# Local q, k and v in products of 32 rows, and an opening in another order

## The chip, the cores and the metric

The kernel runs on one core of a Trainium2 chip. The metric is the device time of one execution in microseconds (us), lower is better. Before the change it is 1029.03 us, the median of three runs (1028.87 to 1030.4).

## The reference, cut to what matters

The input x is four images of 512 rows and 256 columns, all float32. Four steps follow, each on a layer-normed x and added to x:

```
x = x + window_attention(layernorm(x))
x = x + ffn(layernorm(x))
x = x + causal_attention(layernorm(x))
x = x + ffn(layernorm(x))

# window attention: tokens of 16 channels, on a grid of 128 x 64 an image
qkv = tok @ qkv_w                        # 16 -> 48
x1 = branch(first 8 channels of q, k, v, windows of 1 x 8 tokens)
x2 = branch(last 8 channels of q, k, v, windows of 8 x 1 tokens)
# a branch: softmax(q k^T / sqrt 8) v, plus a depthwise 3x3 convolution of v inside the window ("lepe")
att = concat(x1, x2) @ proj_w + proj_b
tok = tok + layernorm(att) * ln_w + ln_b

# ffn: 256 -> 2048 -> 256, 4-bit weights with scales
out = (gelu(x @ Wg.T) * (x @ Wu.T)) @ Wd.T
```

In a window of 1 x 8 only the middle row of a 3x3 filter meets other tokens, in one of 8 x 1 only the middle column: three taps each.

## The kernel before, in words

Five engines work side by side: PE (matrix products), DVE (vector), ACT (activations and copies), POOL, and SP, which only issues transfers. PE's result goes to PSUM, whose banks are handed out from three pools: `pair` gives two banks at once and has two such slots, used in turn; `one` gives a single bank; `fbank` gives the FFN three.

**Stages.** First comes the opening: constants, the window attention of image 0, and the first part of dequantising the FFN's weights. Then come three windows: in each, the first FFN of image b is woven with the window attention of image b + 1 (`beside_window`, L1276; woven by `weave`, L1110). Then the first FFN of image 3 and the second FFN of images 0 to 2 are woven with the causal attention of four images, and the second FFN of image 3 stands alone. The order of PE is written out by hand: `weave` takes a piece of the FFN for each 0.86 us that the other work asks for with its `yield`s, and a factor per window (L1284) stretches these. In the opening (L1196) PE, DVE and ACT all stand in the order of the calls. In the windows the order of DVE and ACT comes from a scheduler, apart from some dependences made by hand (`queue_behind`).

**Local attention of one image.** `window_load` (L223) brings 128 partitions of 8 tokens for each of 8 rows of tokens. `window_front` (L241) takes the statistics, normalises, transposes (`yTp`, L314), copies (`yT`, L321), and multiplies: for each of the 8 rows one product of all 128 rows of partitions (8 tokens of 16 channels) with a block-diagonal weight `bw` of 448 columns (q, k and v of both branches and the first branch's convolution), and one with `taps`, 64 columns for each of the two or three rows of tokens that the second branch's convolution reaches (L334, L336). Each pair of rows goes by one ACT copy into `T` (L344), the taps' bank by one more (L349). For image 0, `busy(12)` (L309) puts products of no use on PE ahead of the transposes. `window_parts` then has, for each branch and half: the products q k (`tq`, L400 and L408), their sum over channels by folds on DVE and by piles on PE (`sc`, L384), the maximum (`mx`), exponent, sums, shares, weighted values (`tv`, L475 and L483), their sum (`va` by PE, L496 by DVE) and `att`. `window_back` projects (`aTp`, L575 and L581; `pr`, `prw`, `ss`), takes the root by Newton steps, forms `z` (L599), which PE moves into the row layout (`zp`, L617), and `add` (L628) adds it to the rows `X`. `rows_shift` (L236) adds the bias ln_b to `X` beforehand, by four ACT operations an image.

**FFN.** `norm_rows` (L680) takes four row statistics (L686), their roots on POOL (`inv_root`, L92 and L93), normalises (`xn`, L700), transposes (`xTp`) and copies (`xT`). `ffn` (L733) has 16 blocks of a gate product (`pg`), an up product (`pu`), gelu on ACT (`gs`) and a product of both on DVE (`it`, L771), and after each eight blocks 32 down products (`po`), added to `X` (L792). All go through the three `fbank` banks, so a later `pg` or `pu` waits until `it` has read an earlier one. `behind_due` keeps the FFN's DVE work behind the image's `add`.

**Weights.** `dequant` (L635 to 668) is a stream of twelve blocks (g0, u0, g1, u1, d0 and so on) of six DVE operations, called words here; `some(words, n)` places n of them, and in window 1 `along` places four at each step of the attention. 24 words stand ahead of the first FFN's transposes.

## Time and profile before

| | us |
|---|---|
| median of three runs | 1029.03 |
| the profiled execution, its own time | 1029.56 |
| its span in the profile | 1027.8 |
| first FFN matmul | 78.33 |
| PE busy, 0 to 76 / 76 to 150 / 150 to the end | 67.97 / 67.24 / 870.83 |
| DVE busy, the same three | 65.52 / 73.90 / 529.86 |
| window 1: first and last piece of image 2's q, k, v | 161.09 to 169.50 |
| window 2: the same of image 3 | 262.9 to 271.85 |

A span is counted from the first to the last event that the profiler sees; the execution's own time has 1.8 us more around it. A row of "busy time by stage" gives a stretch's bounds and length, then for each engine the busy us with the number of instructions (PE, PE's weight loads, DVE, ACT, POOL), the granted clock, the transfer engines' share and GB/s. A group of instructions gives its line, engine, operation, names of output and inputs, shape and count, then busy us and the mean ns of one, then the idle time of that engine just before them and who ended it. [...] the busy times of its groups overlap, and starts tell more than durations. [...]

### The profile page before, as it was taken

Reading aid. Unit: us, or ns where it says so; the run is one execution under the profiler, and the core shown is the slowest. Engines: PE = TensorE matmul, PEld = TensorE weight load, DVE = VectorE, ACT = ScalarE, POOL = GpSimd, SP = SyncE. Lnnn points to the kernel's source line nnn. Section 1 sums busy time; section 2 is a strip of 40 time slices with the busy share of each in tenths; the row PEclk is TensorE's granted clock in tenths of the full one; section 3 lists DMA queues with packets and bytes.
Section 4 is the critical chain, followed back from the end, with each engine's and each line's share of the span. In section 5 each row is a group of like instructions: output and inputs, shape, how many; then the busy total and the mean of one; then the engine's idle time right before and its main releaser. Section 6 shows DMA issues by size and latency. Waiting matters only on the chain.

```text
span 1027.8 us, 13237 instructions
## 1 busy us (share of the span) xinstructions
PE 1006.0 (98%) x5054; PEld 587.9 (57%) x5054; DVE 669.3 (65%) x1570; ACT 350.2 (34%) x586; POOL 133.7 (13%) x261
## 2 busy tenths in 40 slices
PE   7999899999999999999999999999999999999998
PEld 6864656564756475464474554664644746446556
DVE  7989988847776777847477555776465575543111
ACT  2545222131212213435524445235254253461110
POOL 4100100000000012011330112311113201120000
PEclk9999999999999999999999999999999999999999
DMA  7310100000000020000000000000000000000000
GB/s 187 85 40 3 61 21 22 0 1 1 1 1 1 0 68 1 1 1 1 1 1 0 1 2 1 6 16 1 1 1 2 20 1 1 1 1 21 0 1 21
DMA packets 14399, 15.27 MB, mean 15 GB/s; under 512 B 2352, under 2 KB 10840, under 8 KB 14304
## 3 DMA queue, kind: packets, MB, share of 16 engines
q1 hardware_dynamic: 12416, 13.31, 4.4%
q10 hardware_dynamic: 1568, 1.06, 0.4%
q8 instruction: 40, 0.66, 0.3%
q14 instruction: 23, 0.19, 0.1%
q0 software_dynamic: 352, 0.06, 0.1%
HBM read 12.32 MB, written 2.10 MB: 14 GB/s over the span
## 4 chain that ended last, share of the span: by engine, by line
PE 87%; DVE 10%; DMA 1%; POOL 1%; issue 1%; SPq 0%; ACT 0%; ACTq 0%; POOLq 0%; DVEq 0%
PE pg_s L744 11%; PE pu_s L762 11%; PE po_s L779 11%; PE pu_f L762 9%; PE pg_f L744 9%; PE po_f L779 8%; PE s L936 5%; PE o L1021 4%; PE sT L985 4%; PE qkv_b L875 3%; PE qkv L334 2%; PE qkT L912 1%; PE qkv_b L879 1%; DVE tq L408 1%; PE zp L617 1%; DVE tq L389 1%
## 5 line engine op out<-in xcount | busy, mean ns | idle before, releaser
L951 DVE CUSTOM_DVE_ANT_0 junk<-s,mask 128x512 f32<-128x512 f32 (+3 forms) x256 | 110.1, 486 | 36.9 <-PE s L936 19.8
L762 PE MATMUL pu_f<-xT_f,u 128*128 128x512 f32 x256 | 122.9, 597 | 4.4 <-DVE it_f L771 4.1
L744 PE MATMUL pg_f<-xT_f,g 128*128 128x512 f32 x256 | 124.4, 599 | 2.9 <-ACT xT_f L723 1.4
L744 PE MATMUL pg_s<-xT_s,g 128*128 128x512 f32 x256 | 126.7, 603 | 0.0
L762 PE MATMUL pu_s<-xT_s,u 128*128 128x512 f32 x256 | 125.4, 601 | 0.0
L779 PE MATMUL po_f<-d,it_f 128*128 128x256 f32 x512 | 117.5, 381 | 0.6 <-DVE it_f L771 0.6
L779 PE MATMUL po_s<-d,it_s 128*128 128x256 f32 x512 | 118.0, 382 | 0.0
L779 PEld LDWEIGHTS po_s<-d,it_s 128*128 128x128 f32 x512 | 95.2, 190 | 20.8 <-issue 8.8
L779 PEld LDWEIGHTS po_f<-d,it_f 128*128 128x128 f32 x512 | 95.0, 190 | 18.4 <-issue 5.8
L1001 POOL TENSOR_SCALAR_AFFINE_SELECT e<-e 128x256 f32<-128x256 f32 x128 | 52.5, 422 | 344.9 <-ACT e L997 342.1
L997 ACT ACTIVATE e<-sT 128x1024 f32<-128x1024 f32 (+1 forms) x72 | 66.4, 968 | 72.0 <-PE sT L985 72.0
L762 PEld LDWEIGHTS pu_f<-xT_f,u 128*128 128x128 f32 x256 | 47.1, 190 | 61.0 <-issue 51.6
L744 PEld LDWEIGHTS pg_s<-xT_s,g 128*128 128x128 f32 x256 | 45.9, 190 | 56.8 <-issue 50.9
L762 PEld LDWEIGHTS pu_s<-xT_s,u 128*128 128x128 f32 x256 | 46.1, 190 | 54.4 <-issue 50.2
L744 PEld LDWEIGHTS pg_f<-xT_f,g 128*128 128x128 f32 x256 | 46.2, 190 | 53.6 <-issue 42.6
L753 DVE SCALAR_TENSOR_TENSOR g_s<-g_s,gs_s 128x512 f32<-128x512 f32 x48 | 33.1, 691 | 59.1 <-ACT g_s L752 58.5
L756 ACT ACTIVATE gs_f<-pg_f 128x512 f32<-128x512 f32 x48 | 28.5, 595 | 122.4 <-PE pg_f L744 109.7
L771 DVE TENSOR_TENSOR it_f<-pu_f,gs_f 128x512 f32<-128x512 f32 x48 | 32.6, 683 | 33.1 <-PE pu_f L762 33.1
L750 ACT COPY gs_s<-pg_s 128x512 f32<-128x512 f32 x48 | 28.1, 586 | 67.8 <-PE pg_s L744 67.6
L936 PE MATMUL s<-kT,qT 16*128 16x384 f32 (+3 forms) x512 | 50.0, 467 | 0.0
L792 DVE TENSOR_TENSOR X<-po_s,X 128x256 f32<-128x256 f32 (+1 forms) x33 | 13.5, 412 | 54.0 <-PE po_s L779 54.0
L1021 PE MATMUL o<-e,V 128*32 128x256 f32 (+3 forms) x512 | 44.4, 441 | 0.3 <-PE sT L985 0.3
(226 smaller groups left out, 1352.9 us busy)
## 6 DMA issues: line engine op xcount, KB each, us to landing
X<-in_x_dram SPq DMA_DIRECT2D x4, 512.0 KB
out_dram<-X SPq DMA_DIRECT2D x15, 128.0 KB
xa<-in_x_dram SPq DMA_DIRECT2D x28, 64.0 KB
pkg<-in_gate_p_dram SPq DMA_DIRECT2D x4, 256.0 KB
sbg<-in_gate_s_dram SPq DMA_DIRECT2D x4, 256.0 KB
pku<-in_up_p_dram SPq DMA_DIRECT2D x4, 256.0 KB
sbu<-in_up_s_dram SPq DMA_DIRECT2D x4, 256.0 KB
pkd<-in_down_p_dram SPq DMA_DIRECT2D x4, 256.0 KB
```

The source lines that it names most:

```text
L744: nc.tensor.matmul(pg, Wf["g"][par][q][:, o : o + P], xT[:, par, :], start=par == 0, stop=par == 1)
L753: nc.vector.scalar_tensor_tensor(g2, g2, 1.0, gs, ALU.add, ALU.mult)
L762: nc.tensor.matmul(pu, Wf["u"][par][q][:, o : o + P], xT[:, par, :], start=par == 0, stop=par == 1)
L771: behind_due(nc.vector.tensor_tensor(it, pu, gs, ALU.mult))
L779: nc.tensor.matmul(po[:, 0:W], inter[k][:, i * P : (i + 1) * P], Wf["d"][par][j // 2][:, (j % 2) * W : (j % 2 + 1) * W], start=k == 0, sto ...
L875: nc.tensor.matmul(ps[:, 0, :], xT[:, par, rows], c["wqk"][:, :, par], start=par == 0, stop=par == 1)
L936: nc.tensor.matmul(pss[hl // 2][:, hl % 2, at : at + n], qT[h0 : h0 + HD, g, i * P : (i + 1) * P], kT[h0 : h0 + HD, g, 0:n], start=True, s ...
L951: nc.vector.tensor_tensor_reduce(out=junk[:, 0:n], in0=pss[k][:, hl % 2, at : at + n], in1=c["mask"][:, 512 - n : 512], scale=1.0, scalar= ...
L985: nc.tensor.matmul(pss[hl // 2][:, hl % 2, at : at + n], kT[h0 : h0 + HD + 1, g, kt * P : (kt + 1) * P], qT[h0 : h0 + HD + 1, g, kt * P : ...
L997: nc.scalar.activation(e[:, :, 0 : 512 - at0], pss[k][:, :, at0:512], AF.Exp)
L1001: nc.gpsimd.affine_select(out=diag, in_=diag, pattern=[[0, 2], [1, P]], compare_op=ALU.is_ge, fill=0.0, base=0, channel_multiplier=-1,)
L1021: nc.tensor.matmul(outs[g][h0 : h0 + 32, kt * P : 512], v[:, kt, 4 * g + hl, :], e[:, hl % 2, at : at + n], start=kt == 0, stop=kt == 2,)
```

## The change

The weights of q, k and v now cover two tokens instead of eight: `bw` has 96 columns, the same in each group of 32 rows. For each half of an image (`hf`, four rows of tokens) 16 products of 32 rows, four beside each other in four groups of rows and four banks (both `pair` slots), give q, k and v; up to 20 more of 16 to 48 columns give the second branch's convolution in the same banks. After the first half, `across` gives the first branch's convolution by 8 products of all rows and 64 columns. An image has 80 products instead of 16, and `T` is laid out by halves and filled by eight copies and one, whose innermost runs have 2 or 16 elements. The operations of DVE that need both halves of the second branch (`tq` L408 and `tv` L483) become two each. `pw`, `lnw` and `z` use another order of channels.

In the opening, 8 words fewer stand ahead of the first FFN (6 instead of 15 at the first place, 1 more after the first product); `busy(12)` becomes `busy(8)`; image 1's transposes stand behind image 0's second projection instead of ahead of it; the 12 `rows_shift` operations of images 1 to 3 stand ahead of the root instead of after `zp`; image 1's second half stands behind `add`. The first `norm_rows` adds EPS on DVE instead of POOL.

In windows 1 and 2, the first half of the next image's q, k, v and `across` stand ahead of `zp`, the second half behind `add`, with other weights for the weaving. In the built program the causal part has the same order on each engine in both kernels. The second half's second pair of banks follows `zp` in the same slot.

```diff
-        bw = aw.tile([P, 7, 8, 8], F32, name="bw")
...
+        odd = aw.tile([P, 2], F32, name="odd")
+        nc.vector.tensor_reduce(odd, sh[:, 1, :].rearrange("p (r t) -> p t r", t=2), AX.X, ALU.add)
+        bw = aw.tile([P, 96], F32, name="bw")
+        nc.vector.tensor_tensor(
+            bw[:, 0:64].rearrange("p (e t) -> p e t", t=2), bcast(odd, 1, 32), bcast(wrep[:, 0:32], 2, 2), ALU.mult
+        )
...
+        taps = aw.tile([P, 3, 2, 8], F32, name="taps")
+        for t in range(3):
+            nc.vector.tensor_tensor(taps[:, t], bcast(odd, 2, 8), bcast(wc[:, 1, 2 - t, :], 1, 2), ALU.mult)
+        bl = aw.tile([P, 8, 8], F32, name="bl")
...
+        c.update(bw=bw, taps=taps.rearrange("p t j d -> p (t j d)"), bl=bl.rearrange("p j d -> p (j d)"))
...
-            busy(12)
+            busy(8)
...
-        T = a2.tile([P, 8, 8, 8, 8], F32, tag="T", name=f"T{b}")
-        lp = one(f"lepe{b}")
-        for u in range(4):
-            ps = pair(f"qkv{b}_{u}")
-            for a in range(2):
-                s = 2 * u + a
-                nc.tensor.matmul(ps[:, a, 0:448], yT[:, s, :], c["bw"], start=True, stop=True)
-                t0, t1 = (1 if s == 0 else 0), (2 if s == 7 else 3)
-                nc.tensor.matmul(
-                    lp[:, (s - 1 + t0) * 64 : (s - 1 + t1) * 64],
-                    yT[:, s, :],
-                    c["taps"][:, t0 * 64 : t1 * 64],
-                    start=s == 0,
-                    stop=s == 7,
-                    skip_group_check=True,
+
+        T = a2.tile([P, 2, 8, 4, 64], F32, tag="T", name=f"T{b}")
+        state[b] = (y, T)
+
+        def across():
+            lp = one(f"lepe{b}")
+            for s in range(8):
+                nc.tensor.matmul(lp[:, 64 * s : 64 * s + 64], yT[:, s, :], c["bl"], start=True, stop=True)
+            nc.scalar.copy(T[:, :, 7].rearrange("p h s e -> p h (s e)"), lp.rearrange("p (h e) -> p h e", h=2))
+
+        for hf in range(2):
+
+            pss = [pair(f"qkv{b}_{hf}_{k}") for k in range(2)]
+            lo, hi = 4 * hf, 4 * hf + 3
+            for s in range(lo, hi + 1):
+                for r in range(4):
+                    nc.tensor.matmul(
+                        pss[r // 2][:, r % 2, 0:384].rearrange("p (g s e) -> p g s e", g=6, s=4)[:, :, s - lo],
+                        yT[32 * r : 32 * r + 32, s, :],
+                        c["bw"][32 * r : 32 * r + 32, :],
+                        start=s == lo,
+                        stop=False,
+                        skip_group_check=True,
+                    )
+            for s in range(max(lo - 1, 0), min(hi + 1, 7) + 1):
+                t0, t1 = max(0, lo - s + 1), min(3, hi + 2 - s)
+                at = 384 + 16 * (s - 1 - lo)
+                for r in range(4):
+                    nc.tensor.matmul(
+                        pss[r // 2][:, r % 2, at + 16 * t0 : at + 16 * t1],
+                        yT[32 * r : 32 * r + 32, s, :],
+                        c["taps"][32 * r : 32 * r + 32, 16 * t0 : 16 * t1],
+                        start=False,
+                        stop=s == min(hi + 1, 7),
+                        skip_group_check=True,
+                    )
+            for k in range(2):
+                nc.scalar.copy(
+                    T[:, hf, 0:4].rearrange("p g s (d j) -> p (g s d) j", j=8)[:, :, 4 * k : 4 * k + 4].rearrange(
+                        "p n (r t) -> p n r t", t=2),
+                    pss[k][:, :, 0:256].rearrange("p r (n t) -> p n r t", t=2),
                 )
-            nc.scalar.copy(
-                T[:, 0:7, 2 * u : 2 * u + 2].rearrange("p g a j d -> p g a (j d)"),
-                ps[:, :, 0:448].rearrange("p a (g e) -> p g a e", g=7),
-            )
-            yield 0.5
-        nc.scalar.copy(T[:, 7].rearrange("p s j d -> p (s j d)"), lp)
-        state[b] = (y, T)
+            for k in range(2):
+                nc.scalar.copy(
+                    T[:, hf, 4:7].rearrange("p g s e -> p (g s) e")[:, :, 32 * k : 32 * k + 32].rearrange(
+                        "p n (r e) -> p n r e", r=2),
+                    pss[k][:, :, 256:448].rearrange("p r (n e) -> p n r e", e=16),
+                )
+            if hf == 0:
+                across()
+            yield 1.0
...
-                ins = nc.vector.tensor_tensor(
-                    t,
-                    bcast(flat(T[:, 1]), 1, 4),
-                    bcast(T[:, 3, half(hf)].rearrange("p k d j -> p k (d j)"), 2, 8),
-                    ALU.mult,
-                )
+                for sh in range(2):
+                    ins = nc.vector.tensor_tensor(
+                        t[:, :, half(sh)], bcast(T[:, sh, 1], 1, 4), bcast(T[:, hf, 3], 2, 4), ALU.mult
+                    )
...
-        inv_root(rs, mv[:, :, 1])
+        if aside is None:
+            inv_root(rs, mv[:, :, 1])
+        else:
+            nc.vector.tensor_scalar(rs, mv[:, :, 1], EPS, None, ALU.add)
+            nc.gpsimd.tensor_tensor(rs, rs, mhalf[:, 0:4], ALU.pow)
...
-            some(words, 15)
+            some(words, 6)
...
             next(made)
+            some(words, 1)
             next(ahead)
...
             next(first)
             next(second)
             next(first)
-            next(ahead)
             next(second)
             next(second)
             some(ahead, 2)
+            for b in range(1, B):
+                rows_shift(wconst, b)
             drain(turn())
-            some(ahead, 1)
             some(words, 3)
             move()
-            drain(ahead)
-            for b in range(1, B):
-                rows_shift(wconst, b)
             after = [last_on(mybir.EngineType.SP)]
             add()
+            drain(ahead)
             busy(4, wconst["sel"].rearrange("p q h n -> p (q h n)"))
             drain(norm_rows(f1, 0, "f0", got, aside=lambda: some(words, 3)))
...
-            yield from between(scaled(middle, (0.9, 1.36, 1.22)[b - 1]), until(other, state, b + 1))
+            yield from between(scaled(middle, (0.79, 1.24, 1.22)[b - 1]), until(other, state, b + 1))
             project, turn, move, add = window_back(a1, a2, wconst, b, state)
             for hf in range(2):
                 yield from project(hf)
             wait = sum(turn())
             if b + 1 < B:
-                drain(other)
-                wait = 0.9
+                next(other)
+                wait = 3.5
             yield wait
             move()
             yield 0.9
             add()
+            if b + 1 < B:
+                yield 1.4
+                drain(other)
             yield from norm_rows(f1, b, f"f{b}", got, 7.5)
```

## Prediction

> **What bounds the kernel now.** I read the page first (engine shares, slices, chain), then busy time by stage, then the groups of the matmuls touched, then the timeline of the opening and of the first window (the stretch from the first FFN to the second, 78 to 190 us).
>
> ```profile
> span 1027.8 us, 13237 instructions
> PE 1006.0 (98%) x5054; PEld 587.9 (57%) x5054; DVE 669.3 (65%) x1570; ACT 350.2 (34%) x586; POOL 133.7 (13%) x261
> ...
> PE   7999899999999999999999999999999999999998
> ...
> DVE  7989988847776777847477555776465575543111
> ...
> PE 87%; DVE 10%; DMA 1%; POOL 1%; issue 1%; SPq 0%; ACT 0%; ACTq 0%; POOLq 0%; DVEq 0%
> ```
>
> PE is full from the fourth slice on and carries 87% of the chain; DVE's 10% must lie in the first six slices (150 us), where its digits are 7 to 9. The stages say where each rules:
>
> ```profile
> 80.00:150.00 70.00, 64.66 (x198) 36.01 (x197) 69.90 (x104) 22.98 (x56) 3.32 (x3) 1.00 0.09 31
> 100.00:110.00 10.00, 5.91 (x14) 2.22 (x13) 10.00 (x15) 1.19 (x2) 0.00 (x0) 1.00 0.15 48
> ...
> 150.00:160.00 10.00, 10.00 (x42) 5.63 (x41) 4.51 (x8) 2.88 (x5) 0.00 (x0) 1.00 0.00 1
> 180.00:275.00 95.00, 93.88 (x396) 55.82 (x398) 68.30 (x99) 24.79 (x39) 1.95 (x2) 1.00 0.00 0
> 275.00:370.00 95.00, 94.98 (x483) 58.84 (x472) 69.37 (x111) 16.71 (x25) 1.82 (x4) 1.00 0.03 6
> ```
>
> The second number is PE, the fourth DVE. From 80 to 150 DVE has no rest (69.90 of 70) and PE stands for 5.3 us; PE's waits put most of that down to one pair:
>
> ```profile
> PE pu_f L762 <- DVE it_f L771: 4.1, 2, 3.3
> ```
>
> (us, times, longest). From 150 PE is full and DVE has slack. So three prices hold: before 76 us a step counts if it is on the opening's chain; from 76 to 150 each us of DVE can push PE; after 150 each us of PE counts once.
>
> ```profile
> L334 PE MATMUL qkv<-bw,yT 128*128 128x448 f32 x64 | 29.6, 544 | 0.4 <-ACT yT L321 0.4
> L936 PE MATMUL s<-kT,qT 16*128 16x384 f32 x128 | 16.3, 533 | 0.0
> L617 PE MATMUL zp<-z,sel 128*32 128x128 f32 x512 | 14.8, 273 | 0.1
> L336 PE MATMUL lepe<-taps,yT 128*128 128x192 f32 x48 | 11.7, 326 | 0.0
> L936 PE MATMUL s<-kT,qT 16*128 16x128 f32 x128 | 7.6, 270 | 0.0
> ```
>
> These busy numbers overlap, so I price by starts in the timeline. [...]
>
> **1. The products.** Before, an image takes 8 x 448 + 1408 = 4992 columns. Image 2's ran from 161.09 to 169.50: 8.41 us, 1.68 ns a column. After: 32 matmuls of 96 columns on 32 rows, 40 of 16 to 48 columns on 32 rows, 8 of 64 columns on all rows (the part across), in two halves of four token rows, hf0 and hf1. The nearest row is s (L936): four matmuls on 16 rows each, one bank each, which start within some 7 ns of each other; four of 384 and four of 128 columns take 1.07 us together, and rounds of four 128-column passes follow each other by 109 ns. So, with two passes a matmul and four passes a round: 16 rounds for q, k, v, 20 for the taps, 16 single passes for the part across, 52 x 0.109 = 5.7, with turns between shapes 5.9 us. Saved 2.5 us an image.
>
> [...] The row says a round cannot pass 109 ns at 128 columns and shows nothing narrower. I take 109 for all: taps of 16 columns cost a full round. Bounds: 1.5 us saved (rounds at 130 ns) and 4.8.
>
> Four images save, but image 0's and 1's lie in the opening (see 3). On the full PE lie images 2 and 3: -2.5 each, **-5.0 us**.
>
> **2. Copies and splits.** An image's ACT copies were 4 x 0.91 + 0.59 = 4.2 us (128x896 and 128x512). Now 4 x 512 elements (0.59) and 4 x 384 (0.48 on the slope of those two) plus 0.59: 4.9, if runs of two elements cost no more; no row shows such runs. Bounds 4.9 and 9 (double). ACT is 34% busy; only the opening's first scores see it. Two branch-1 operations per half are split: 2.20 becomes 2 x 1.13, +0.06, four times an image: +0.24 of DVE. z's other order: 0 to -0.1 each (bounds -0.4, 0).
>
> **3. Opening.** First FFN matmul: 78.33. The chain into it: q, k, v from 16.68; the first product (22.92) behind 9 words of dequantisation; score piles to 39.86; attention to 53.66; projection, root, z at 64.64 and 66.34; zp 65.86 to 69.5; add 69.62 to 70.84; norm_rows: last statistics 73.1, POOL root 73.55 to 75.0, xn 75.04; ACT's copies at 77.70, behind 12 row statistics of images 1 to 3 (72.91 to 77.7).
> After: hf0 needs 2.9 us, its copies 1.7, so the first product starts near 19.1; hf1 waits for the pair banks those copies free; second product near 23.5 (before 26.13). Less DVE work stands ahead of the scores (8 words later), so the first maximum comes near 29.4 instead of 32.47: -3.05. The projection no longer stands behind image 1's transposes (56.98 to 58.07): -0.55. EPS on DVE removes a POOL step, -0.25. Statistics done earlier: -0.4 of the copies' wait. Against this, hf1 of image 1 now stands between zp and the FFN, its second bank pair frees only with the add, and busy(4) (3.45 us) stands behind it: I put the first FFN matmul at 74.7: **-3.6**. If copies are slow: up to +1.
> busy(12) to busy(8): in the trace passes of this chain start 213 ns apart until 15.27, then 109, though the granted clock reads 1.00. [...] here it took 6.4 (from 8.92, with 24 passes). [...] by the trace eight leave hf0 at half rate, +1.35 on that chain. I take half of it as in my -3.6 already, and keep 0 to +1.35.
>
> **4. Window 1: where the eight words go.** A block of six is 3.07 us, two more 2 x 0.60: 4.27 us of DVE are removed from ahead of the FFN and must be done in 76 to 150, where DVE is full. So DVE finishes its window work at about the old time, whatever the opening gained. The up products waiting for it_f to free a bank would show it first. In the changed order of DVE the eleventh it_f stands behind branch 1's attention output (before, ahead of tv's last sums), so the down/gate run that waits for it begins near 148.3 instead of 145.34: **+3.0** relative to before, the opening's -3.6 included; that is, 6.6 us more PE waits in window 1, the splits among their cause. Bounds: 0 (PE finds other matmuls, DVE idles less) and +4.5 (the words beside an unchanged opening).
>
> **5. The tail of window 1.** hf0 goes before zp, hf1 behind the add, since its second bank pair is zp's. In before, z_1 ends 167.85, zp 170.4 to 174.1, add 175.88 to 177.06, late because DVE first does the statistics of image 3 (whose loads landed after 172). After: z_1 near 167.2, zp 167.9 to 171.6, add done near 176.4; po or hf1's first part fills PE to 174.2, then PE waits 2.1 us; behind hf1 all FFN matmuls queue. At the same place of the work PE then stands at +3.0 + 2.1 - 2.5 (image 2) = +2.6: the saving pays for the wait. The FFN f1 starts with 0.3 instead of 1.1 us of waiting (192.5 and 196.6 before): **+1.8**. Bounds of the wait: 0 and 4 (as long as DVE's late statistics hold the add, 172 to 176).
>
> **6. Window 2 and after.** Image 3's products: -2.5, with 0.4 of new waiting at its hf1 (there the add is not held by statistics of a next image). Window 3, the causal part and the last FFN have the same order: 0. Prologue constants are smaller (fewer columns to build) but in the time of the loads: 0 (bounds -0.5, +0.3); X and image 1's loads now stand ahead of u0's words on SP: hidden, or up to +1 in the opening.
>
> **Sum.** +1.8 - 2.5 + 0.4 = **-0.3 us** on the profiled execution's 1029.56 (span 1027.8 and 1.8 around it): 1029.3. The median of the runs shown is 1029.03, 0.53 lower, so I predict 1028.7.
>
> **The rivals.**
> - *Both savings survive (faster).* DVE idles less, PE finds other matmuls while it_f is late, and the opening's 3.6 us are worth as much as the eight words cost. For: PE has 5.3 us of waits in 80 to 150 that an earlier start could fill. Against: 69.90 of 70. Window 1 at 0 instead of +3.0, and hf1's wait filled: 0 - 5.0 + 0.4 = -4.6, 1024.4.
> - *The add gate (slower).* hf1 shares a bank pair with zp, so it waits on PE for the add, and every FFN matmul stands behind it. With window 1 at +3.0 and f1's -0.8, the two images' -5.0 bear 2.8 us of waits together; beyond that the kernel is slower than before. For: the add of window 1 comes 1.8 us after zp's end, behind statistics. At 4 us in each window: +3.0 - 0.8 - 5.0 + 8.0 = +5.2, 1034.2.
> - *The change does not do what it says.* Row-packed passes follow each other at 54 ns, not four in 109: 144 x 0.054 + 1.7 = 9.5 us, +1.1 an image instead of -2.5. That is 7.2 more for two: +6.9, 1035.9. The row of s speaks against it.
>
> **How the numbers follow.** About 0.2%, 2.06 us, is what a measurement of this kernel can tell from no change. The likeliest case, gains paid back in window 1, holds 0.34: 1027.0 to 1031.1, its own range. Faster 0.31 (1023 to 1027). Slower 0.35: the add gate 0.26, no packing 0.09 (1031 to 1037). The range leaves out about 0.1 at each end: 1023 to 1036.
>
> **What would show it.** Step 1: image 2's products in some 5.9 us between first and last start, rounds near 109 ns. 3: first FFN matmul near 74.7, first maximum near 29.4. 4: DVE still full to 150, and PE's waits from 76 to 150 up by some 6 us. 5: PE idle before the second half of image 2's products for about 2 us, released by the add. Wrong if those rounds take over 150 ns, if window 1's waits do not grow (then it is near 1024), or if ACT's small runs cost double.

## The result, and the profile after

The changed kernel takes 1041.1 us (median of four runs, 1039.41 to 1042.87) beside 1029.72 for the kernel before: ratio 1.0111, 95% interval 1.0086 to 1.0136. It is slower by 11.4 us; 1028.7 was forecast, 1036 the end of the range. The profiled execution took 1039.41, its span is 1037.6.

From the page of the kernel after, the lines that answer to those of before, and the granted clock of PE by slices:

```profile
span 1037.6 us, 14293 instructions
PE 1010.1 (97%) x5558; PEld 599.9 (58%) x5558; DVE 669.0 (64%) x1588; ACT 353.6 (34%) x604; POOL 132.9 (13%) x260
...
PE   7989899999999999999999999999999999999998
...
DVE  5889998829784877846586655666465575543111
...
PEclk7999999899999999999999999999999999999999
```

Before, the last of these lines was:

```profile
PEclk9999999999999999999999999999999999999999
```

PE is busy 4 us longer although its products became shorter, and PEclk now has a 7 and an 8. DVE's first digit fell from 7 to 5: it stands idle in the opening, as the stretch from 16 to 32 us shows before and after (columns as before: the third pair is DVE, the last three numbers are the granted clock, the transfers' share and GB/s):

```profile
16.00:32.00 16.00, 15.77 (x68) 11.73 (x67) 15.04 (x22) 8.30 (x23) 0.56 (x2) 1.00 0.83 232
16.00:32.00 16.00, 16.00 (x163) 14.84 (x158) 6.71 (x10) 7.38 (x25) 0.00 (x0) 0.53 0.88 257
```

Busy time by stage, after:

```profile
80.00:150.00 70.00, 61.55 (x188) 34.50 (x187) 69.55 (x105) 26.19 (x63) 2.67 (x3) 0.95 0.10 33
100.00:110.00 10.00, 6.55 (x12) 2.56 (x11) 10.00 (x16) 1.66 (x6) 0.00 (x0) 0.83 0.01 2
150.00:160.00 10.00, 10.00 (x30) 4.71 (x29) 9.48 (x18) 2.38 (x4) 0.00 (x0) 1.00 0.05 18
180.00:275.00 95.00, 93.48 (x450) 59.71 (x449) 66.61 (x113) 24.25 (x42) 2.84 (x3) 0.96 0.00 1
275.00:370.00 95.00, 94.97 (x495) 58.08 (x494) 69.78 (x108) 18.55 (x29) 1.21 (x2) 1.00 0.00 1
```

The clock's changes, read from the same trace, are at 13.82, 30.89, 68.43, 71.84, 105.98, 109.39, 136.70, 140.11, 184.49 and 191.31: five stretches of half rate, 34 us together, of which a busy PE loses half (from 15.4 to 16.5 us rounds of 96 columns follow each other by 213 ns, at full rate, in image 3's products, by 112). All their lengths are multiples of 3.41 us: three of 3.41, one of 6.83 (two) and one of 17.07 (five). Before, the trace records full rate from 15.3 us to the end of the span, and nothing ahead of 15.3. That is one execution: the same code, run as the first part of probe and of probe2 below, has 10.2 and 6.8 us of half rate, and takes 69.5 and 67.2 us from the first FFN matmul to gate block 12 instead of 67.0. A difference of up to some 3 us between two single traces can be of this kind. Stages of the changed kernel cut at its changes of the clock:

```profile
14.00:31.00 17.00, 17.00 (x175) 15.72 (x174) 8.61 (x13) 7.50 (x23) 0.74 (x2) 0.50 0.81 234
31.00:68.00 37.00, 33.10 (x237) 28.75 (x235) 33.18 (x47) 16.92 (x48) 3.85 (x3) 1.00 0.07 25
...
184.50:191.30 6.80, 6.80 (x37) 5.63 (x34) 4.61 (x10) 1.84 (x4) 1.21 (x2) 0.50 0.00 0
```

From 14 to 31 us PE never rests (17.00 of 17) and still stays at half rate: there run hf0, the part across and hf1 of image 0, and from 26.6 the first score piles.

Where the 9.8 us of the profiled execution lie is read by setting the same FFN block of both traces side by side (start after minus start before):

| place | before | after | difference | forecast |
|---|---|---|---|---|
| first FFN matmul (end of the opening) | 78.33 | 82.55 | +4.2 | -3.6 |
| gate block 12 of f0 (window 1) | 145.3 | 155.6 | +10.3 | +3.0 |
| first gate block of f1 | 188.9 | 202.4 | +13.5 | |
| gate block 4 of f1 (window 1 paid) | 204.5 | 216.3 | +11.8 | +1.8 |
| gate block 4 of f2 (window 2 paid) | 304.1 | 313.8 | +9.7 | -0.3 |
| everything later | | | +9.7 | -0.3 |

(Blocks count from 0 to 15; what the expectations below call the seventh gate block is this block 12.) So the opening lost 7.8 us more than forecast, window 1 up to block 12 the same as forecast (+6.1 instead of +6.6), its tail 2.7 more (+1.5 instead of -1.2), and window 2 gained just what was forecast (-2.1). Products and copies of the changed kernel:

```profile
L344 PE MATMUL qkv<-bw,yT 32*128 32x96 f32 x256 | 12.3, 318 | 3.9 <-DVE X L655 2.5 <-DVE ss L97 1.5
L356 PE MATMUL qkv<-taps,yT 32*128 32x32 f32 x128 | 9.0, 299 | 0.0
L356 PE MATMUL qkv<-taps,yT 32*128 32x48 f32 x128 | 7.1, 318 | 0.0
L356 PE MATMUL qkv<-taps,yT 32*128 32x16 f32 x64 | 4.1, 270 | 0.0
...
L365 ACT COPY T<-qkv x16: 586/589/592, 18.8 to 285.9; 128x512 f32<-128x512 f32 x16
L371 ACT COPY T<-qkv x16: 497/504/510, 19.7 to 286.7; 128x384 f32<-128x384 f32 x16
```

(The last two lines are of the tile's view: minimum, median, maximum ns.) Copies in runs of two elements cost 0.59, as much as long runs (L336's copies of the same size, 128x512, take 0.59 too). From the first start of a piece to the start of what follows it, image 3's products took 2.1 us for hf0, 1.8 for the part across and 2.1 for hf1: 6.1 against 8.4 before (263.28 to 271.69; the 262.9 to 271.85 in the table of before counts from the first weight load to the end of the last product).

### The profile page after: what moved, and what is told of

Read it like the earlier page. It is cut to its first block, busy times and chain, and to the rows that moved or that the text cites. A ratio compares the mean times of both kernels' runs of the same rounds, so it can differ in the third digit from the quotient of the medians.

```text
span 1037.6 us, 14293 instructions
## 1 busy us (share of the span) xinstructions
PE 1010.1 (97%) x5558; PEld 599.9 (58%) x5558; DVE 669.0 (64%) x1588; ACT 353.6 (34%) x604; POOL 132.9 (13%) x260
## 4 chain that ended last, share of the span: by engine, by line
PE 87%; DVE 9%; DMA 1%; issue 1%; SPq 0%; POOL 0%; ACT 0%; POOLq 0%; ACTq 0%; DVEq 0%
PE pg_s L775 11%; PE pu_s L793 11%; PE po_s L810 11%; PE po_f L810 10%; PE pg_f L775 9%; PE pu_f L793 9%; PE s L967 5%; PE o L1052 4%; PE sT L1016 4%; PE qkv_b L906 3%; PE va L412 2%; PE qkT L943 1%; PE qkv_b L910 1%; PE zp L644 1%; DVE tq L437 1%; PE qkv L356 1%
## 5 line engine op out<-in xcount | busy, mean ns | idle before, releaser
L793 PE MATMUL pu_f<-xT_f,u 128*128 128x512 f32 x256 | 125.3, 605 | 3.5 <-DVE it_f L802 3.5
L810 PE MATMUL po_f<-d,it_f 128*128 128x256 f32 x512 | 120.5, 388 | 1.9 <-DVE it_f L802 1.8
L810 PEld LDWEIGHTS po_f<-d,it_f 128*128 128x128 f32 x512 | 96.9, 194 | 21.4 <-issue 5.2
L781 ACT COPY gs_s<-pg_s 128x512 f32<-128x512 f32 x48 | 28.2, 587 | 67.7 <-PE pg_s L775 67.5
L823 DVE TENSOR_TENSOR X<-po_s,X 128x256 f32<-128x256 f32 (+1 forms) x33 | 13.5, 413 | 54.0 <-PE po_s L810 54.0
```

The source lines that it names most:

```text
L793: nc.tensor.matmul(pu, Wf["u"][par][q][:, o : o + P], xT[:, par, :], start=par == 0, stop=par == 1)
L810: nc.tensor.matmul(po[:, 0:W], inter[k][:, i * P : (i + 1) * P], Wf["d"][par][j // 2][:, (j % 2) * W : (j % 2 + 1) * W], start=k == 0, sto ...
```

## The experiments

Two theories were set against each other at first. **C**: the packed products do not count as work for whatever grants PE its clock, so PE falls to half rate in the midst of work. **O**: the order (weights later, hf1 behind the add, less ahead of the first scores) makes the waits. Both turned out to hold a part. Medians follow, with the ratio to the kernel before, measured beside them on the same chip, and its 95% interval.

**probe.** The kernel before, with stretches of useless products after its last output product:

```diff
+        warm(0)              # 12 products of 512 columns on all rows
+        packed(1, 70, 96)    # 280 products: 32 rows, 96 columns, four beside each other
+        warm(1)
+        packed(2, 70, 32)
+        warm(2)
+        whole(3, 70, 64)     # all rows, 64 columns
+        warm(3)
+        whole(4, 70, 128)
+        warm(4)
+        packed(5, 20, 384)
```

> The kernel before, unchanged, with stretches of useless products on PE after its last output product: 280 packed on 32 rows and 96 columns (four groups of rows beside each other), 280 packed with 32 columns, 70 on all rows with 64 columns, 70 on all rows with 128 columns, 80 packed with 384 columns, each after 12 products of 512 columns on all rows. Theory C (packed products do not count as work for the clock's gate, so PE falls to half rate although it never rests): in the 96 and 32 column stretches rounds of four passes start 109 ns apart for at most 6.8 us and 213 ns apart from then on, granted clock 0.5; the 128 column stretch stays at 1.00; 64 columns are open. Rival O (only rest and order matter): PE never rests here, the granted clock is 1.00 in all stretches and rounds stay at 109 ns.

The five stretches, in this order, by stage:

```profile
1038.20:1053.70 15.50, 15.50 (x557) 15.50 (x560) 0.00 (x0) 0.00 (x0) 0.00 (x0) 1.00 0.02 4
1064.50:1090.20 25.70, 25.70 (x561) 25.64 (x560) 0.00 (x0) 0.00 (x0) 0.00 (x0) 0.59 0.01 3
1102.10:1117.50 15.40, 15.40 (x140) 15.40 (x139) 0.00 (x0) 0.00 (x0) 0.00 (x0) 1.00 0.00 1
1128.00:1143.50 15.50, 15.50 (x141) 15.50 (x140) 0.00 (x0) 0.00 (x0) 0.00 (x0) 1.00 0.00 1
1154.00:1167.00 13.00, 13.00 (x161) 8.10 (x160) 0.00 (x0) 0.00 (x0) 0.00 (x0) 1.00 0.01 1
```

Theory C as it stood was wrong in half: 96 columns packed keep the full rate (560 passes in 15.6 us, 112 ns a round of four). The narrow ones lose it: of the 32 column stretch the clock fell at 1069.22, 4.8 us in, and stayed at half to its end, though PE never rested. In these stretches packing was not the cause, narrowness was: at full rate a round of 32 columns still takes 112 ns, of which 32 columns stream for some 27 (an estimate: image 2's 4992 columns took 8.41 us in two passes before, 0.84 ns a column and pass). So in the changed kernel the taps (16 to 48 columns) are suspect.

**order_alone** (the old products in the new order), **products_alone** (the new products in the old order), **busy22** (22 useless products ahead of image 0's transposes):

```diff
-                        yT[32 * r : 32 * r + 32, s, :],   # order_alone: per hf, two times
+                nc.tensor.matmul(ps[:, a, 0:448], yT[:, s, :], c["bw"], start=True, stop=True)
...
-            some(words, 6)        # products_alone
+            some(words, 15)
...
-            busy(8)               # busy22
+            busy(22)
```

> The changed kernel with the old products of all rows (448 columns and taps of 64) and the old layout of T, in two halves at the places of hf0 and hf1; all of the new order stays. Theory C: the granted clock stays at 1.00 from the first warm stretch of the opening to 180 us, apart from rests of PE over 2 us; the first FFN matmul comes before 80 (82.55 in the changed kernel), the total is near 1034 (the 4.7 us of new waits of the prediction, no saving of products). Rival O: the loss of the order remains and the saving is gone: 1043 to 1046.

> The new products, copies and split operations in the old order: busy(12), 15 words at the first place, rows_shift after zp, POOL's EPS, both halves ahead of zp, the old factors of the weaving. Theory C: half rate in the opening while the packed products of images 0 and 1 run, first FFN matmul at 80 to 83 instead of 78.3, and again around images 2 and 3 if they meet a rest; total 1029 to 1034. Rival O: clock 1.00 throughout as in the kernel before, opening 2 to 3 us earlier, both later images 2.5 us shorter: 1022 to 1025.

> The changed kernel with 22 instead of 8 useless products ahead of image 0's transposes, so that PE does not rest there (2.83 us in the changed kernel). Theory C: the clock still falls to 0.5 while hf0, the part across and hf1 of image 0 run, at the latest 6.8 us after hf0 begins, and comes back only in the score piles; first FFN matmul within 1.5 us of 82.55, total 1037 to 1042. Rival (the rest before the transposes alone sets the gate): clock 1.00 from there on, first FFN matmul near 78, total near 1034.

order_alone took 1038.27 (1.0065, 1.0046 to 1.0085), at half rate for only 6.8 us after its warming: neither 1034 nor 1043. products_alone took 1035.88 (1.0062, 1.0039 to 1.0085); its profiled execution, at 1040.42 one of the three slowest of eight, has half rate in five stretches, among them 64.95 to 78.6 around image 1's products and zp. The order alone loses 8 us, the products alone 5.5, together 11.4: they overlap. busy22 took 1038.29 (1.0078, 1.0057 to 1.0099): with no rest ahead of the transposes the clock held to 21.94, 3 us into image 0's products, and then fell all the same until 32.18. So the rest was not needed for the fall; it set only its beginning. The first FFN matmul stayed where it was, at 82.7.

**late_word, words15, wide_taps, words15_wide** take single pieces out of the changed kernel:

```diff
-            some(words, 1)        # late_word: moved to the next some(words, 2)
...
-            some(words, 6)        # words15, and no some(words, 1)
+            some(words, 15)
...
-                        pss[r // 2][:, r % 2, at + 16 * t0 : at + 16 * t1],   # wide_taps
+                        pss[r // 2][:, r % 2, at + 16 * t1 - 96 : at + 16 * t1],
...
-                        c["taps"][32 * r : 32 * r + 32, 16 * t0 : 16 * t1],
+                        c["wide"][32 * r : 32 * r + 32, t0, 80 + 16 * t1 - 96 : 80 + 16 * t1],
```

> The changed kernel with its one early word (the first of u0, behind which DVE stood 4.6 us for u0's load) two places later, behind branch 1's first product. Theory D (that word's wait holds the second product, all scores and so the opening): the second product starts near 24.5 instead of 28.2, as soon as hf1's copies let it, first FFN matmul 3 to 4 us earlier than 82.55, total 1036 to 1038. Rival (half rate of PE alone holds the opening: hf1 ends at 26.7 and its copies at 27.9 anyway): second product at 27.9, first FFN matmul within 1 us of before, total 1040 to 1042.

> The changed kernel with the words of before ahead of the scores: 15 at the first place, none after the first product; the products, the order of PE and hf1's places stay. Theory W (the words moved into the full DVE of window 1 cost what they were reckoned at, and DVE stands idle instead while T is made): DVE busy from 16 to 32 us at 14 or more instead of 6.7, from the first FFN matmul to the seventh gate block +1 to +2 instead of +6.4 against before, total 1031 to 1034. Rival C (half rate alone): DVE fuller, but the same total within 1.5 us of 1041.

> The changed kernel with each taps product widened to 96 columns by zero columns of weights ahead of its own, which add nothing to their neighbours in the bank; a round still takes its 109 ns. Theory C as the probe leaves it (packed products of 32 columns count too little, 96 are enough): the granted clock stays or comes back to 1.00 while the products run, half rate after 20 us at most one stretch of 3.4 us per rest of PE, products of images 2 and 3 as long as before the widening; opening 1 to 2 us earlier, total 1036 to 1039. Rival (any packed product, or the rests alone): stretches of half rate as in the changed kernel, 1039 to 1043.

> Both of the last two edits. If W and C are separate and both hold: the sum of their gains, 1026 to 1031. If the half rate was only a consequence of PE's rests behind DVE: the same as the words alone, within 1 us.

late_word: 1040.34 (1.0092, 1.0062 to 1.0122), not to be told from the changed kernel. The second product came at 28.0, after 28.2 in the changed kernel: with u0's word gone, the next small step in DVE's queue, the constants made from proj_b, stood for its own load. DVE's waits in late_word:

```profile
DVE bm L206 <- DMA pbrow<-in_proj_b_dram: 4.0, 1, 4.0
```

and in the changed kernel:

```profile
its engine sat idle before it (us, times) until:
  DMA pku<-in_up_p_dram: 4.6, 1
```

Theory D, one word, was too narrow: whatever DVE does first after the first product waits for transfers that now stand with 2 MB of X and image 1's rows. The rival (half rate holds hf1's copies) gave the right number for late_word, but not the reason: there the copies that the product needs were done at 24.85. In the changed kernel the two limits end together, the load at 27.86 and those copies at 27.85.

words15: 1037.35 (1.0065, 1.0044 to 1.0087); DVE's 16 to 32 us are full again, 14.2 instead of 6.7. But from the first FFN matmul to gate block 12 it still lost 4.7 us (+6.7 to +11.4 in its trace), so theory W failed on window 1. wide_taps: 1037.67 (1.0077, 1.0054 to 1.01), in its profiled execution (1035.72, the fastest of four) half rate after 20 us in two stretches, 6.8 and 3.4 us, instead of 28 us in all: C as the probe left it holds, for 3.4 us. Both together: 1034.13 (1.0044, 1.003 to 1.0059): 7.0 off 1041.1, beside 3.8 and 3.4. In the medians the gains add.

In the trace of words15_wide, PE's longest wait in the opening beside its start shows a new one:

```profile
PE sc L418 <- DVE tq L434: 3.1, 1, 3.1
```

The products are done sooner than DVE can use them; PE rests from 23.25 to 26.35, and the next stretch of half rate (27.48 to 30.89) falls on the score piles.

**hf1_early, fill, fill_early, products_fill.** fill puts three useless products of 512 columns into that rest, on top of words15_wide; hf1_early drains hf1 ahead of zp in the changed kernel; the other two combine.

```diff
             drain(front)
+            busy(3, wconst["sel"].rearrange("p q h n -> p (q h n)"))     # fill
...
             some(words, 3)
+            drain(ahead)                                                 # hf1_early
             move()
...
-                next(other)
-                wait = 3.5
+                drain(other)
+                wait = 0.9
```

> The changed kernel with hf1 of images 1, 2 and 3 ahead of zp, directly after hf0 and the part across, so that it no longer waits for the add. The prediction's step 5 and its rival, the add gate: PE's waits for the add (2.5 us in two waits in the changed kernel) vanish, and with them the rest before the half rate at 184 to 191 us; from the seventh gate block of f0 to the first of f1 +0.5 or less instead of +3.2 against before; total 1037 to 1039. Rival (the add gate costs nothing of note because packed products and rests earlier set the gate): within 1 us of 1041, or the half rate only moves to another place.

> The changed kernel with wide taps and the 15 words, and with three useless products of 512 columns between hf1 of image 0 and the score piles, where PE rested 3.1 us for DVE's first product in the run without them. Theory C: no half rate in 23 to 34 us, the piles at full rate, first FFN matmul 2 to 3 us earlier than 83.0, total 1031 to 1033. Rival (the opening is held by DVE and ACT, PE's rate there is free): first FFN matmul within 0.7 us of 83.0.

> All four edits: wide taps, 15 words, the three fillers, hf1 ahead of zp. If the causes are separate their gains add: about 3.4 + 3.8 + 1.5 + 2 off 1041, 1028 to 1031, at or a little below before.

> The new products with wide taps in the old order of everything, and the three fillers ahead of the score piles. Theory C: the whole loss of the new products in the old order (5.5 us) was half rate; with it gone the products of images 2 and 3 save their 1.9 us each: 1025 to 1028. Rival: something else of the new products (copies in small runs, split operations, longer program) costs as much: 1030 to 1034.

fill: 1032.84 (1.003, 1.0019 to 1.0042), full rate from 13.46 on but for one stretch, first FFN matmul at 78.7 instead of 83.0. Between these two traces the three products, which compute nothing, are worth 4.3 us at that place; the medians differ by 1.3, so not every execution gains as much. hf1_early was a miss: 1049.83 (1.0189, 1.0173 to 1.0205). PE's wait in it:

```profile
PE zp L644 <- ACT T L371: 2.8, 1, 2.8
```

zp needs a pair of banks that ACT's copies of hf1 must free, and in the new order these copies stand behind the twelve rows_shift operations (72.18 to 77.07 on ACT); the opening grew by another 11 us (1.5 of them earlier than this), with half rate from 67.26 to 84.33. In windows 1 and 2 the waits for the add were gone, but so was image 3's saving (+21.6 to +21.4 from gate block 4 of f1 to that of f2). fill_early shows the same: 1042.32 (1.0117, 1.0103 to 1.0132), zp resting 4.5 us. hf1 behind the add is the better place. products_fill: 1032.79 (1.0031, 1.0018 to 1.0043), half of the loss of products_alone; in my arrangement hf1 stood ahead of zp here too, and zp again waited (1.6 us) and ran at half rate, so what the new products would do in the old order at full rate stays open.

**fill_pace, fill_pace1, old_pace, old_words6.** At fill, the opening was even with before (+0.3) and window 1 still lost 6.3 us up to block 12.

```diff
-            yield from between(scaled(middle, (0.79, 1.24, 1.22)[b - 1]), until(other, state, b + 1))
+            yield from between(scaled(middle, (0.9, 1.36, 1.22)[b - 1]), until(other, state, b + 1))   # fill_pace
+            yield from between(scaled(middle, (0.9, 1.24, 1.22)[b - 1]), until(other, state, b + 1))   # fill_pace1
```

old_pace is the kernel before with 0.79 and 1.24, old_words6 the kernel before with 6 and 1 words at the places of the changed one.

> The run with wide taps, 15 words and fillers, with the old factors of the weaving in windows 1 and 2 (0.9 and 1.36 instead of 0.79 and 1.24). Theory P (the new factor lets window 1's attention come earlier on PE, and DVE, which is full, gets to it's products late, so PE rests more): from the first to the seventh gate block of f0 +1 to +3 instead of +6.3 against before, total 1027 to 1030. Rival (split operations and the halves' order on DVE): still +5 or more in that stretch, total 1031 to 1034.

> The same with the old factor in window 1 alone (0.9, 1.24). Theory P: as fill_pace in window 1; window 2 keeps the 1.9 us of image 3's products; total 1027 to 1030. Rival: 1031 to 1034.

> The kernel before with the new factors of the weaving alone. Theory P: window 1 loses 3 us or more by the seventh gate block of f0, total 1032 to 1035. Rival: within 1.5 us of before.

> The kernel before with 6 instead of 15 words at the first place and 1 after the first product, as in the changed kernel: eight words deferred, nothing else. The prediction's step 4: opening 2 to 4 us earlier if the early word does not wait for its load, window 1 losing 4 to 7 us up to the seventh gate block; total +1 to +4, 1031 to 1034. If the early word waits for u0's load behind X and image 1 (4.6 us in the changed kernel): opening not earlier, total +4 to +7.

old_pace: 1035.72 (1.0058, 1.0037 to 1.0078). Two numbers in one line cost the kernel before 5.4 us. Its trace is even with before at the first FFN matmul (-0.3) and +4.9 at block 12. Its PE waits:

```profile
PE pu_f L762 <- DVE it_f L771: 3.6, 1, 3.6
PE po_f L779 <- DVE it_f L771: 3.1, 3, 1.6
PE pg_f L744 <- DVE X L792: 3.1, 2, 2.5
```

Before, the first pair had 4.1 and the second 0.6. With the smaller factor fewer FFN pieces are woven into each step of the attention, and PE comes back to the FFN at places where DVE, which is full, has not yet made `it`; one rest (97.38 to 100.99) went with 6.8 us of half rate, from 100.05 on. fill_pace: 1030.47 (1.0016, 1.0 to 1.0033), block 12 at +0.1; fill_pace1: 1028.69 (0.999, 0.9972 to 1.0009). Theory P holds: with the old factor window 1 loses nothing up to block 12 (+0.4 to +0.1 in fill_pace's trace, +9.9 to +9.6 in that of fill_pace1). Both spread from 1026 or 1028 up to 1038 or 1039: the profiled execution of fill_pace1, 1037.58, had half rate from 15.58 to 32.65 and from 70.2 to 77.0, and its first FFN matmul at 88.25, where fill with the same opening had it at 78.67.

old_words6: 1039.99 (1.0093, 1.0074 to 1.0112). Its DVE waits up to 80 us:

```profile
DVE bm L198 <- DMA pbrow<-in_proj_b_dram: 3.8, 1, 3.8
DVE tq L400 <- ACT T L344: 3.5, 1, 3.5
```

The first FFN matmul came at +4.7, block 12 at +5.9, so the deferred words cost 4.7 in the opening and 1.2 in window 1 (with 3.4 us of half rate in each), the reverse of the forecast. The rest of its loss is a rest of 3.1 us in f1 and half rate from 205.7 to 212.5.

**probe2, fill_busy14.** What brings the clock back, and the best version with a longer warming:

```diff
+        packed(1, 60, 32)     # probe2: to half rate, then
+        packed(2, 60, 96)     # likewise whole 64, whole 128, packed 384
...
-            busy(8)               # fill_busy14: fill_pace1 with
+            busy(14)
```

> The kernel before with stretches after its last output product. Each begins at half rate, brought about by 240 packed products of 32 columns (12 us or more), followed by one kind: 240 packed of 96 columns, 60 whole of 64, 60 whole of 128, 80 packed of 384, with products of 512 columns between. Theory H (keeping the clock takes less work than getting it back): full rate returns within 6.8 us under whole 128 and packed 384, but not, or much later, under packed 96 and whole 64, which kept it in the first probe. Rival (one threshold): it returns within 6.8 us under all four.

> fill_pace1 with 14 instead of 8 useless products ahead of image 0's transposes. If a rest there (2.3 us in the profile of fill_pace1 that took 1037.58) lets the clock fall just as the packed products begin, and these cannot bring it back: fewer executions above 1032, median 1027 to 1028.5. [...] spread and median as fill_pace1, 1028.7.

Cut at the clock's own changes, packed 96, whole 64, whole 128 and packed 384 from half rate:

```profile
1057.30:1061.50 4.20, 4.20 (x80) 4.20 (x83) 0.00 (x0) 0.00 (x0) 0.00 (x0) 0.50 0.00 0
1061.60:1072.80 11.20, 11.20 (x406) 11.18 (x402) 0.00 (x0) 0.00 (x0) 0.00 (x0) 1.00 0.02 4
1104.20:1129.80 25.60, 25.60 (x123) 25.60 (x121) 0.00 (x0) 0.00 (x0) 0.00 (x0) 0.50 0.00 1
1163.30:1167.30 4.00, 4.00 (x23) 4.00 (x20) 0.00 (x0) 0.00 (x0) 0.00 (x0) 0.50 0.00 0
...
1210.00:1215.10 5.10, 5.10 (x32) 3.27 (x36) 0.00 (x0) 0.00 (x0) 0.00 (x0) 0.50 0.00 0
1215.20:1225.60 10.40, 10.40 (x132) 6.73 (x124) 0.00 (x0) 0.00 (x0) 0.00 (x0) 1.00 0.01 2
```

Three kinds return to full rate, after 4.1 to 5.2 us. Whole products of 64 columns do not within 25.6 us, though the first probe kept full rate under them for 15.4. Theory H is right for whole products of 64 columns and wrong for packed 96. The packed products of 32 columns lost full rate each of the four times, after 3.3 to 5.6 us. The part across is made of whole products of 64 columns: in the changed kernel it fills 3.7 us of image 0's products at half rate (19.0 to 22.7), and through it and the taps on both sides the clock stayed at 0.50.

fill_busy14: 1027.78 (1025.6 to 1028.31 in seven runs; 0.9972, 0.9961 to 0.9984). It is faster than both kernels, 0.28% under the one before. Beside fill_pace1 the intervals overlap; what differs is the spread, with none of seven executions above 1028.31 where three of fourteen were above 1032. Its opening by stage:

```profile
16.00:32.00 16.00, 16.00 (x197) 13.48 (x198) 14.79 (x23) 7.37 (x25) 0.00 (x0) 1.00 0.83 251
32.00:76.00 44.00, 38.97 (x429) 32.60 (x428) 41.09 (x66) 23.38 (x60) 4.95 (x4) 1.00 0.11 37
```

PE at full rate, DVE full: first FFN matmul -1.4, block 12 -0.1, gate block 4 of f1 +0.2, of f2 -1.75. Image 2's saving goes into hf1's wait for the add (1.75 us) and f1's start; image 3's 2.0 us are what remains.

## Why the prediction was wrong

**Step 1, the products: right in mechanism, 0.2 us too large.** Rounds of four passes at full rate take 112 ns in the probe, and taps of 16 columns cost a full round (two of image 3's start 112 ns apart in the changed kernel), as was taken from the row of s, with its 109 ns at 128 columns. The bound of 4.8 us was an estimate of mine that no row showed. 6.1 us instead of 5.9 an image: saved 2.3, not 2.5; window 2 gained 2.1 (+11.8 to +9.7). The rival "does not do what it says" is refuted. But here the narrow sides cost more than a round's time: wide_taps, which streams nearly three times the columns in rounds of 105 ns, has 10.2 us of half rate after 20 us instead of 28 and takes 3.4 us less.

**Step 2: right.** 0.59 and 0.50 us for the copies, against 0.59 and 0.48.

**Step 3, the opening: the step that failed, by 7.8 us.** The first product came at 19.9 (19.1 forecast), but the second at 28.2, not 23.5, and the first maximum at 36.07, not 29.4. Three terms of the sum failed:
- "Less DVE work stands ahead of the scores ... -3.05." DVE did not gain the eight words' time, it stood idle: 6.7 us busy of 16 instead of 15.0. old_words6 shows this alone at +4.7.
- "X and image 1's loads now stand ahead of u0's words on SP: hidden, or up to +1": DVE waited 4.6 us. The nine words had hidden all those loads. I named the cover and did not price it at what the words themselves took.
- "busy(12) to busy(8) ... keep 0 to +1.35": the clock was lost for 17 us. I priced a delayed warming, from the one case the trace had (passes 213 ns apart until 15.27; the 1.00 of its first 15.3 us stands for no record of the clock); a rest of 2.8 us ahead of narrow products was not priced, nor the products themselves, under which busy22 lost the clock without that rest.

The loads and the clock cannot be added, for each hides the other. The traces side by side (half rate is counted from 16 us to the first FFN matmul):

| run | words at the first place | half rate, us | first FFN matmul |
|---|---|---|---|
| before | 15 | 0 | 78.33 |
| after | 6 | 18.3 | 82.55 |
| busy22 | 6 | 10.2 | 82.71 |
| late_word | 6 | 7.8 | 82.28 |
| wide_taps | 6 | 7.2 | 82.55 |
| fill | 15 | 0 | 78.67 |
| words15_wide | 15 | 10.2 | 83.03 |
| words15 | 15 | 16.8 | 85.01 |
| fill_pace1 | 15 | 23.5 | 88.25 |

With the words away, 8 to 11 us less of half rate do not bring the first FFN matmul forward. In late_word and wide_taps hf1's copies for the second product were done at 24.9 and 24.2, and DVE still stood for the loads until 27 and 28 us; PE then rested for 3.0 and 4.2 us, and the half rate that came fell on the score piles. (busy22 begins its products 2.7 us later.) With the words back, the end of the opening goes with the half rate, over 9.6 us; fill and fill_pace1 have the same opening. So words15 alone, and wider taps alone, left the opening as late as it was or later: their gains of 3.8 and 3.4 us lie behind it, and only both with the fillers brought it back, in an execution that kept the clock.

In each trace that has several, all stretches of half rate begin on one grid of 3.41 us and last multiples of it. In the changed kernel their starts, 13.82, 68.43, 105.98, 136.70 and 184.49, lie 16, 11, 9 and 14 steps apart. What sets the grid was not shown.

**Step 4, window 1: the right size from the wrong cause.** +6.6 was forecast, as waits for the deferred words; +6.1 was measured. From the first FFN matmul to block 12, before and after:

```profile
78.33:145.34 67.01, 61.66 (x191) 34.79 (x192) 66.94 (x98) 23.59 (x61) 3.32 (x3) 1.00 0.09 32
82.55:155.63 73.08, 65.30 (x190) 35.86 (x191) 72.63 (x112) 26.75 (x64) 2.67 (x3) 0.95 0.10 33
```

PE's rests grew by 2.4 us (5.3 to 7.8), not by some 6, and 6.8 us of half rate came on top, worth up to 3.4. old_pace, where the factors alone changed, has the same two amounts, 7.7 us of rests and 6.8 of half rate, and loses 5.3 us there; old_words6 loses 1.2. The factors were in the diff, and the prediction left them out. That its number was met is luck.

**Step 5, the tail: the waits right, what follows them missed.** PE waited 1.5 us in window 1 for the add (2.1 forecast) and not at all in window 2 (0.4). But the rest of 1.5 us beside narrow products was followed by half rate from 184.49 to 191.31, where PE is full: some 3.4 us, about the 2.7 by which this step was off. The runs with the same factors and hf1 behind the add bear this out: the three traces with half rate there (after, late_word, busy22) have the step at +1.5 to +1.7, the four without it (wide_taps, words15, words15_wide, fill) at -0.7 to -1.8, around the -1.2 forecast. In words15 a rest as long (1.5 us), beside the same narrow products, passed without a loss.

**Step 6: right in its sum.** -2.1 in window 2, with no wait, instead of 2.5 less 0.4: a saving put a little too large and a wait that did not come, which cancel by luck. The same order later gives the same time.

**The rivals.** The add gate was put forward as the slower case, 1034. It is real but small (1.0 us in the opening and 1.5 in window 1), and hf1 ahead of it is worse. The slower case that came, loads without cover, a factor of the weaving and half rate, stood in the text as two bounds of the opening instead of as a rival, and the factor not at all.

How the 11.4 us divide can be told only for single edits, since they overlap: on the kernel before, the words cost 9.7, the factors 5.4 and the products 5.5; taken back from the changed kernel one on the other, wide taps and words give 7.0 (1041.1 to 1034.1), fillers 1.3 by the medians (1032.8), window 1's factor 4.2 (1028.7), the longer warming 0.9 (1027.8). The steps of 1.3 and 0.9 are not clear of the spread of these runs. What stays open: why image 3's saving is lost with hf1 ahead of zp, and the new products in the old order at full rate.

## What to carry to other kernels

A step that gives work back to a full engine later must be priced at both ends: what the moved work had been hiding (here loads and 8 us of idle DVE) and what it meets. Every constant of a hand-made order is part of the change: two factors alone cost the kernel before 5.4 us. A limit that is mended while another of the same length stands beside it can show no gain, as in this opening, so mend both before calling one harmless. Where PE is packed with narrow products or gets a rest of a few us (here half rate followed some rests of 1.5 to 3.6 us, and not others), look at the granted clock of each stage before its busy time: here widening products by zero columns was worth 3.4 us, more than the 2.1 that the shorter products saved in window 2.

## What the runs showed of the hardware

- Full rate was lost while PE was 100% busy: 32 columns on four groups of rows lost it in 3.3 to 5.6 us, in each of five stretches; 96 and 384 columns packed, and 64 and 128 on all rows, kept it for 13 to 15.6 us (one stretch each).
- Whole products of 64 columns kept full rate for 15.4 us in probe and did not regain it in 25.6 us in probe2; packed 96, whole 128 and packed 384 regained it there in 4.1 to 5.2 us. At 0.84 ns a column and pass, an estimate from these runs (8.41 us for 4992 columns in two passes), 32 columns stream for 27 of a round's 112 ns, 64 for 54 of a pass's 110, 96 for 81 of 112. So what kept full rate streamed for about half of the time or more, what lost it for a quarter, and what regained it for nearly three quarters or more. Whether this share or the number of columns is what counts was not shown.
- Rests of like length ended differently, and the traces differ in where the rest lay on the grid of 3.41 us. The kernel before has one rest of 3.3 us ahead of an up product of window 1. In its profiled execution it lay 1.9 and 1.5 us in two steps of the grid (105.6 to 108.9) and nothing was lost. In probe and probe2 2.7 and 2.4 us of it lay in one step, and 6.8 and 3.4 us of half rate began at the end of that step (110.07, 109.25). A rest of 1.5 us in a step of the changed kernel, whose other part was filled with narrow products, was followed by half rate too (181.5 to 183.0, half rate from 184.49).
- ACT copies in runs of two elements took as long as those in long runs (0.59 us for 128x512 in both).
- A float32 product stands in the traces as two passes (the 280 packed products of 96 columns in probe as 560 weight loads and 557 matmuls), and passes overlap: the 64 of L334, 544 ns each on average, 34.8 us together, fill 29.6 us in the kernel before.
